# Key and value projections of a second cross-attention in row tiles, pass ends reordered, a last softmax divided late

## The chip, the cores and the metric

The kernel runs on one core of a Trainium2 chip. A core has TensorE (matrix products, results in PSUM), VectorE, ScalarE and GpSimd, and SyncE, whose queue issues most of the transfers from memory. In the profile they are PE (PEld is the loading of weights into TensorE), DVE, ACT, POOL and SP. Every engine runs its own list of instructions in order and waits for others by semaphores. The metric is the device time of one execution in microseconds (us).

## What is computed

`x` is 128 latent rows of 256; the context `ctx` has 12544 rows of 192. Six blocks follow each other, each added to `x`:

```
x = x + cross_attention_0(layernorm(x), ctx)   # 16 heads of 16, then an MLP
x = x + causal_attention(layernorm(x))
x = x + experts_0(layernorm(x))                # 8 experts, top 2
x = x + cross_attention_1(layernorm(x), ctx)   # 16 heads of 64
x = x + attention_1(layernorm(x))
x = x + experts_1(layernorm(x))                # 8 experts, top 2
```

The change is in the fourth and fifth. The fourth is

```
q, k, v = x @ Wq, ctx @ Wk, ctx @ Wv           # Wq 256x1024, Wk and Wv 192x1024
sim  = einsum('bhid,bhjd->bhij', q, k) * 64**-0.5
out  = einsum('bhij,bhjd->bhid', softmax(sim), v)
return out @ Wo + bo
```

and the fifth is

```
probs = softmax(x @ x.T / 16)
vac   = where(probs < 0.01, probs, 0)
sp    = probs - vac;  sp = sp / (sum(sp) + 1e-9)
return sp @ x + 0.01 * (sum(vac) broadcast to 256) @ W.T
```

All of it is float32.

## The kernel before

The context is taken in 13 superblocks of 1024 rows (the last has 256). In the second cross-attention (`with tc.tile_pool(name="l1x"...)`, from L898) two heads make a pass, so there are 8 passes. A period is one superblock of one pass, 104 in all: `periods[t] = (j, s)`. A period projects the keys of its superblock (192 rows of weights to 128 columns, two heads), computes the scores of all 1024 keys with 128 queries and two heads, and keeps them in SBUF; 14 periods later (`LAG`), when the pass's maximum is known, they are shifted by the maximum, exponentiated, summed, and multiplied with the values, which are projected shortly ahead.

The 192 rows of the contraction do not fit TensorE's 128 rows. `load_context` brings the first 128 rows as one tile `lo` (1024 columns), and the last 64 as a tile `hi`, whose upper 64 partitions hold the first half of the superblock's columns and whose lower 64 the second half. `project_keys` and `project_values` work on two PSUM banks, one for each half `r` of the superblock. `tiled()` multiplies the 64 rows of `hi`: two products on the two 64-row halves of the array, side by side, one for each bank (L213 for keys, L231 for values). `whole(r)` multiplies the 128 rows of `lo` on the whole array, one bank after the other (L216, L238). `ahead` says which of the two starts the accumulation. Keys come as two products of 512 columns a half, values as products of 128 columns. In the profile each float32 product is two instructions, so x32 at L980 are 16 products, that is 8 pairs of heads.

Most periods are run two at a time by `two_periods(t)`, for t = 12, 14, ... 100, under a manual schedule: the order in which its calls are written is each engine's order. A call handles, on TensorE: attention of the two periods that are 14 back (`attend`, L1098, on 128x64 tiles), scores of t (`scores`, L980, on 64-row tiles), projections of keys for t + 1 and values, scores of t + 1, with a second set of projections for t + 2 between them. The first set is tiled and then whole, the second whole and then tiled. Beside it: `keeping` gives the copy of the scores to SBUF (L997, ScalarE) and the running maximum (L1004, VectorE); `shift` adds the negative maximum (L1071, GpSimd, or VectorE when `beside`); `exponent` is L1082 on ScalarE; `added` sums over keys on VectorE (L1125) and adds these on GpSimd (L1130) through a ring of three `part` tiles; `taken` adds attention's product to an accumulator (L1142). Keys are copied out of PSUM in halves, half 0 by VectorE (L953) and half 1 by ScalarE (L951), and values by ScalarE (L965).

PSUM holds two double banks for scores and a ring of four single banks (`ps_w`) for all else here: two for keys, two for values, and those of attention, of the transposes at the end of a pass and of the sums. A tile takes a bank that was given back, so the product waits for the reader before it.

At the end of a pass, `fold` reduces the running maximum (L1034, VectorE), `pass_maximum` transposes it (L249) and reduces it again, and `pass_spread` transposes it back over the partitions (L254), into a bank which ScalarE copies to SBUF (L1051) and from which VectorE's `shift` reads directly. The end of a pass falls in the first half of a double (`ends`) or in the second (`ends_later`, followed by a double that `begins`). In the double that begins, the first attention of the new pass used a scores' bank (`late`).

Weights of keys and values for all passes are loaded at the start by `context_weight` (`ywk`, `ywv`), 1024 columns each. A context load is three issues on SP's queue (L194, L196) into two rotating buffers, in the tail every third one into slots of a ring of 28 tiles.

After the last scores comes a tail (t = 104 to 117), in which a period is attention (into `final["both"]`), a projection of values and the exponentials. At t = 107 four products with `ones` and `awT` (L1327) compute the column sums of W that the next block needs. That block (from L1411) runs on one tile: its softmax is divided, masked, summed, divided again, transposed and multiplied. Then the experts (from L1454) follow, whose weights are 24 loads of 512 KB into ring slots.

## Time and profile before

| what | value |
|---|---|
| median of 4 runs | 1570.05 us (1568.65 to 1574.32) |
| profiled execution | 1571.0 us, span 1569.3 us |
| PE busy | 1487.4 us, 95% of the span |
| DVE, ACT, POOL busy | 1156.8, 987.4, 858.2 us |
| mean granted clock of TensorE | 0.989 |
| mean DMA throughput | 93 GB/s |

The second cross-attention begins at about 571 us of the span and ends at about 1505; its paired periods run from 616 to 1426 us. A line of the timeline gives the start in us from the span's beginning, the length, the engine, the line of the kernel, the operation, what it writes and reads, its shape, how many such instructions follow each other, and in brackets the idle time of the engine before it with the instruction that ended it. A line of the chain of waits gives start, length, engine, tile and line. Lengths of matrix products include a modelled end that overlaps the next one, so the distance between starts tells what one took.

### The profile page before, as it was taken

How to read it: one execution, taken by the hardware profiler on the slowest of the kernel's cores; microseconds unless marked ns; L12 is line 12 of the kernel's file. 1: busy time of each engine (PE TensorE's matmuls, PEld its weight loads, DVE VectorE, ACT ScalarE, POOL GpSimd, SP SyncE). 2: the span in 40 equal slices, each digit the busy share in tenths (PEclk: the TensorE clock that was granted, in tenths of full speed). 3: DMA queues.
4: the chain of work that ended last, by engine and by line, in shares of the span. 5: the costliest groups of instructions: out<-in, count | busy, mean ns of one | idle time of the engine just before them, and what ended most of it. 6: DMA issues, size and time to landing. Idle time of an engine off the chain costs nothing.

```text
span 1569.3 us, 39688 instructions
## 1 busy us (share of the span) xinstructions
PE 1487.4 (95%) x17138; PEld 1150.8 (73%) x17138; DVE 1156.8 (74%) x1226; ACT 987.4 (63%) x1233; POOL 858.2 (55%) x563
## 2 busy tenths in 40 slices
PE   7999989999879999999999999999999999999979
PEld 4666656666645877887787887787887788888968
DVE  3899887999883327777778876778876878778742
ACT  4899988999883236665565655565655565555541
POOL 0488878988840000763874663864663864764300
PEclk9999999999999999999999999999999999999979
DMA  3111021211086860332223332223322223224680
GB/s 105 44 61 42 27 62 42 62 43 42 14 240 191 267 169 18 98 97 70 82 82 89 96 86 67 81 82 96 93 82 69 80 83 105 82 82 134 186 282 4
DMA packets 68737, 146.62 MB, mean 93 GB/s; under 512 B 8905, under 2 KB 27089, under 8 KB 68562
## 3 DMA queue, kind: packets, MB, share of 16 engines
q1 hardware_dynamic: 68258, 143.30, 31.0%
q8 instruction: 135, 2.21, 0.6%
q10 hardware_dynamic: 304, 0.79, 0.2%
q14 instruction: 40, 0.33, 0.1%
HBM read 143.92 MB, written 0.13 MB: 92 GB/s over the span
## 4 chain that ended last, share of the span: by engine, by line
PE 62%; DVE 7%; ACT 4%; POOL 3%; issue 2%; DMA 1%; DVEq 0%; ACTq 0%
PE x_s L980 11%; PE x_v L238 10%; PE x_k L216 9%; PE x_o L1098 8%; PE x_v L231 5%; PE x_k L213 5%; POOL x_p L1071 2%; PE f_h L1469 2%; PE f_h L842 2%; PE f_py L859 2%; PE x_both L1098 1%; PE k L216 1%; DVE x_part L1125 1%; ACT x_p L525 1%; POOL x_p L514 1%
## 5 line engine op out<-in xcount | busy, mean ns | idle before, releaser
L1071 POOL TENSOR_TENSOR x_p<-x_p,x_spread 128x1024 f32<-128x1024 f32 x179 | 410.2, 2327 | 206.3 <-ACT x_spread L1051 206.3
L514 POOL TENSOR_TENSOR x_p<-x_p,x_spread 128x512 f32<-128x512 f32 (+1 forms) x184 | 324.4, 1812 | 127.0 <-ACT x_spread L502 65.1
L1125 DVE TENSOR_REDUCE x_part<-x_p 128x256 f32<-128x1024 f32 (+1 forms) x175 | 327.9, 1914 | 18.5 <-POOL x_sums L1130 10.4
L997 ACT COPY x_p<-x_s 128x1024 f32<-128x1024 f32 (+1 forms) x200 | 198.9, 1001 | 206.8 <-PE x_s L980 105.4
L1130 POOL TENSOR_TENSOR x_sums<-x_sums,x_part 128x256 f32<-128x256 f32 x161 | 117.4, 729 | 255.2 <-DVE x_part L1125 254.3
L1004 DVE TENSOR_TENSOR x_mx<-x_s,x_mx 128x1024 f32<-128x1024 f32 (+1 forms) x161 | 193.3, 1201 | 79.1 <-PE x_s L980 58.9
L449 ACT COPY x_p<-x_s 128x1024 f32<-128x1024 f32 x196 | 193.5, 1016 | 50.6 <-PE x_s L436 35.5
L238 PEld LDWEIGHTS x_v<-ywv_lo,x_ctx_lo 128*128 128x128 f32 x1568 | 190.0, 192 | 39.6 <-issue 36.1
L1082 ACT ACTIVATE x_p<-x_p 128x1024 f32<-128x1024 f32 (+1 forms) x200 | 204.6, 1048 | 17.8 <-POOL x_p L1071 13.7
L525 ACT ACTIVATE x_p<-x_p 128x1024 f32<-128x1024 f32 x196 | 196.5, 1063 | 0.2 <-DVE x_p L514 0.2
L238 PE MATMUL x_v<-ywv_lo,x_ctx_lo 128*128 128x128 f32 x1568 | 195.4, 276 | 0.2 <-ACT x_v L965 0.2
L455 DVE TENSOR_TENSOR x_mx<-x_s,x_mx 128x1024 f32<-128x1024 f32 x140 | 168.1, 1221 | 33.0 <-PE x_s L436 18.2
L980 PE MATMUL x_s<-x_qT,x_kT 64*128 64x128 f32 x2744 | 175.5, 277 | 11.5 <-ACT x_p L997 9.5
L980 PEld LDWEIGHTS x_s<-x_qT,x_kT 64*128 64x128 f32 x2744 | 161.7, 188 | 21.0 <-ACT x_p L997 11.2
L216 PE MATMUL x_k<-x_ctx_lo,ywk_lo 128*128 128x512 f32 (+1 forms) x364 | 167.3, 582 | 0.0
L1098 PE MATMUL x_o<-x_p,x_v 128*64 128x128 f32 x2744 | 160.9, 274 | 0.1
L1098 PEld LDWEIGHTS x_o<-x_p,x_v 128*64 128x64 f32 x2744 | 148.7, 137 | 6.4 <-issue 0.4
L231 PEld LDWEIGHTS x_v<-ywv_hi,x_ctx_hi 64*128 64x128 f32 x1568 | 104.2, 188 | 42.9 <-issue 41.6
L436 PE MATMUL x_s<-x_qz,x_kT 32*128 32x256 f32 x1568 | 118.6, 403 | 17.7 <-ACT x_p L449 16.6
L965 ACT COPY x_v<-x_v 128x512 f32<-128x512 f32 (+1 forms) x208 | 108.4, 565 | 32.0 <-PE x_v L238 24.5
L538 PE MATMUL x_o<-x_p,x_v 128*32 128x128 f32 x3136 | 113.7, 279 | 9.9 <-ACT x_p L525 9.0
L538 PEld LDWEIGHTS x_o<-x_p,x_v 128*32 128x32 f32 x3136 | 83.1, 110 | 54.3 <-ACT x_p L525 20.0
(268 smaller groups left out, 1788.2 us busy)
## 6 DMA issues: line engine op xcount, KB each, us to landing
x_ctx_lo<-in_ctxT_dram SPq DMA_DIRECT2D x119, 512.0 KB, 4.0
x_ctx_hi<-in_ctxT_dram SPq DMA_DIRECT2D x238, 128.0 KB, 3.9
f_w<-in_L_ffn_W_dram SPq DMA_DIRECT2D x32, 512.0 KB, 5.1
k_lo<-in_ctxT_dram SPq DMA_DIRECT2D x12, 512.0 KB, 8.5
f_gating<-n_kernel_gating_EDF_dram SPq DMA_DIRECT2D x8, 512.0 KB, 10.4
f_up<-L_ffn_kernel_up_EDF_dram SPq DMA_DIRECT2D x8, 512.0 KB, 10.0
f_wd<-ffn_kernel_down_EFD_dram SPq DMA_DIRECT2D x8, 512.0 KB, 10.1
k_hi<-in_ctxT_dram SPq DMA_DIRECT2D x24, 128.0 KB, 7.7
```

The source lines that it names most:

```text
L216: nc.tensor.matmul(ps[r][:, :h], wk[0][:, js], lo[:, r * h : (r + 1) * h], start=not ahead, stop=ahead)
L238: nc.tensor.matmul(ps[r][:, kc * P : (kc + 1) * P], lo[:, r * h + kc * P : r * h + (kc + 1) * P], wv[0][:, js], start=(not ahead and kc == ...
L449: nc.scalar.copy(ps[t][k], st[k].rearrange("p a n -> p (a n)"))
L514: engine.tensor_tensor(v, v, by[:, banks].unsqueeze(2).to_broadcast([P, n, 2, 256]), ALU.add)
L525: nc.scalar.activation(ps[t][k], ps[t][k], AF.Exp)
L538: nc.tensor.matmul(os[b][32 * i : 32 * i + 32, u * P : (u + 1) * P], v[:, 2 * g + c, 17 * (2 * i + u) : 17 * (2 * i + u) + 32], p[i // 2][ ...
L980: nc.tensor.matmul(st[:, u, c * P : (c + 1) * P], kTs[t][rs, ks], qT[rs, j, :], start=True, stop=True)
L997: nc.scalar.copy(scores_kept(ps[t][i], sts[i].shape[2] // P), sts[i])
L1071: engine.tensor_tensor(v, v, by.unsqueeze(2).to_broadcast([P, 2, n, P]), ALU.add)
L1082: nc.scalar.activation(v, v, AF.Exp)
L1098: nc.tensor.matmul(o[us, 0:P], vs[t][:, c0 + c, us], p[:, n0 : n0 + P], start=(c0 + c == 0 and (s == 0 or not whole)), stop=(c0 + c == tot ...
L1125: nc.vector.tensor_reduce(part, v, AX.X, ALU.add)
```

## The change

Projections of keys and values in the second cross-attention are made wholly of 64-row products. A context tile now has 128 partitions of three pieces: the upper 64 partitions hold the 192 rows of the first half of the superblock as three pieces of 64, the lower 64 those of the second half. A projection has three steps; in a step, the two halves are multiplied side by side, each on its half of the array and into its own bank. Context tiles rotate through three buffers, in the tail too. Weights are loaded by pass, both halves of the partitions holding the same three pieces, one pass ahead.

In the double periods the first set's keys and then values run whole, the second set's too; the copies of keys out of PSUM are placed anew. In the doubles that end or begin a pass, `pass_maximum` and `pass_spread` stand between keys, the first step of values, and the other two; a second shift is done by VectorE; sums of exponentials are placed later; `fold` of the doubles that end later is moved to the next one; the late attention uses an ordinary bank after the second values. The column sums of W leave the tail and are computed after the attention's residual, into a bank of their own. In the next block the masked probabilities are transposed and multiplied before their division, which comes with the last addition; the discarded part is computed by GpSimd.

```
+    def load_rows(t, ap):
+        nc.sync.dma_start(t, ap.rearrange("(c p) n -> p c n", p=64))
+
+    def load_context_rows(pool, name, s, bufs):
+        k0 = s * SB
+        h = min(SB, SK - k0) // 2
+        t = pool.tile([P, 3, KB], F32, tag="ctx", name=name, bufs=bufs)
+        for r in range(2):
+            load_rows(t[64 * r : 64 * r + 64, :, :h], a["ctxT"][:, k0 + r * h : k0 + (r + 1) * h])
+        return t, h
+
+    def project_keys_in_rows(name, w, cx):
...
+        def go(i):
+            for r in range(2):
+                rs = slice(64 * r, 64 * r + 64)
+                nc.tensor.matmul(ps[r][:, :h], w[rs, i, :], t[rs, i, :h], start=(i == 0), stop=(i == 2))
...
+    def project_values_in_rows(name, w, cx):
...
+        def go(i):
+            for kc in range(h // P):
+                ks = slice(kc * P, (kc + 1) * P)
+                for r in range(2):
+                    rs = slice(64 * r, 64 * r + 64)
+                    nc.tensor.matmul(
+                        ps[r][:, ks], t[rs, i, ks], w[rs, i, :], start=(i == 0 and kc == 0), stop=(i == 2),
...
-        ywk = context_weight(work, "ywk", a["L1_xattn_Wk"])
-        ywv = context_weight(work, "ywv", a["L1_xattn_Wv"])
+        def load_pass_weight(kind, j):
+            if j < NH // 2 and (kind, j) not in weights:
+                t = work.tile([P, 3, P], F32, tag="yw" + kind, name=f"yw{kind}{j}", bufs=2)
+                for r in range(2):
+                    load_rows(t[64 * r : 64 * r + 64], a["L1_xattn_W" + kind][:, j * P : (j + 1) * P])
+                weights[kind, j] = t
...
-            place = slot if t >= NP and (t - NP) % 3 == 2 else None
-            ctxs[t] = load_context(work, f"x1_ctx{t}", (t + 1) % NS, 2, place=place)
+            ctxs[t] = load_context_rows(work, f"x1_ctx{t}", (t + 1) % NS, 3)
...
+            if begins:
+                fold(j)
             context(t)
...
-            k[0]()
-            v[0]()
+            whole(k)
             copy, maximum = keeping(t, sts)
             copy(0)
             if begins or ends:
...
+                out(k)
                 pass_maximum(j)
-                v[1](0)
+                whole(v, 0)
                 pass_spread(j)
-                v[1](1)
-                for r in range(2):
-                    v[2](r)
-                first, second = (b[1], nx) if begins else (nx[0], nx[1:])
-                shift(first, 0, True)
-                shift(first, 1)
-                for u in second:
-                    shifted(u)
-                exponents(first)
-                if begins:
-                    summed(2, first)
-                    exponents(nx[0])
-                    summed(1, nx[0])
-                else:
-                    summed(3, first)
+                whole(v, 1, 2)
+                out(v)
+                first = [(u, i) for u in (b[1:] + nx if begins else nx) for i in range(2)]
+                for i in (0, 2):
+                    shift(*first[i], True)
+                for u, i in first:
+                    shift(u, i)
+                for u, i in first[:2]:
+                    exponent(u, i)
             else:
-                for f in (k, v):
-                    for r in range(2):
-                        f[1](r)
+                whole(v)
...
+            k, v = keys(t + 2), values(t + 2 - NS)
+            whole(k)
+            if ends:
+                summed(2, nx[0])
+                exponent(nx[1], 0)
+                out(k)
+                summed(1, nx[1])
+            elif begins:
+                summed(2, b[1])
+                exponent(nx[0], 0)
+                out(k)
+                exponent(nx[0], 1)
+                summed(1, nx[0])
+            else:
+                out(k)
+            whole(v)
             if begins:
-
-                late = attend(b[1], ps_s(f"x1_o{b[1]}")[:, 0])
...
+                o = attend(b[1])
+                taken(b[1], o)
+            out(v)
+            if not begins and not ends and at != NS - 3:
                 summed(1)
...
                 if t == NP + 3:
-
-                    for c in range(2):
-                        nc.tensor.matmul(
-                            final["both"][:, 1, D : 2 * D], ones, awT[:, c, :], start=(c == 0), stop=(c == 1)
-                        )
                     projected(0, PASSES - 1)
...
-            wsum = final["both"][:, 1, D : 2 * D]
+            pc = ps_mm("a1_pc")
+            for c in range(2):
+                nc.tensor.matmul(pc[:, :D], ones, awT[:, c, :], start=(c == 0), stop=(c == 1))
...
         sp = work.tile([P, P], F32, name="a1_sp")
-        nc.vector.tensor_tensor(sp, pr, vac, ALU.subtract)
+        nc.vector.scalar_tensor_tensor(sp, pr, 0.01, pr, ALU.is_ge, ALU.mult)
+        pt = ps_t("a1_spT_ps")
+        nc.tensor.transpose(pt[:, 0:P], sp, ident)
...
-        spn = work.tile([P, P], F32, name="a1_spn")
-        nc.vector.tensor_scalar(spn, sp, rs, None, ALU.mult)
-        spT = transposed(work, spn, 1, "a1_spT", tag="spT")
+        spT = work.tile([P, P], F32, name="a1_spT")
+        nc.vector.tensor_copy(spT, pt[:, 0:P])
...
+        nc.gpsimd.tensor_tensor(vac, pr, sp, ALU.subtract)
...
+        x = xp.tile([P, D], F32, tag="x", name="x5")
+        nc.vector.scalar_tensor_tensor(x, pa[:, :D], rs, y, ALU.mult, ALU.add)
```

## The prediction

> **What bounds the kernel now.** I read the page first: busy times, then the chain that ended last.
>
> ```profile
> PE 1487.4 (95%) x17138; PEld 1150.8 (73%) x17138; DVE 1156.8 (74%) x1226; ACT 987.4 (63%) x1233; POOL 858.2 (55%) x563
> PE 62%; DVE 7%; ACT 4%; POOL 3%; issue 2%; DMA 1%; DVEq 0%; ACTq 0%
> ```
>
> TensorE is the bound, and the changed attention (571 to 1505 us of the span) is most of it. Next I read TensorE's timeline of one ordinary double (two periods by `two_periods`): start, length, engine and line, tiles.
>
> ```profile
> 1034.53 2.06 PE L980 MATMUL x_s<-x_qT,x_kT 64*128 64x128 f32 x32
> 1036.42 1.03 PE L213 MATMUL x_k<-x_ctx_hi,ywk_hi 64*128 64x512 f32 x4
> 1037.28 1.06 PE L231 MATMUL x_v<-ywv_hi,x_ctx_hi 64*128 64x128 f32 x16
> 1038.26 1.98 PE L216 MATMUL x_k<-x_ctx_lo,ywk_lo 128*128 128x512 f32 x4
> 1040.09 1.95 PE L238 MATMUL x_v<-ywv_lo,x_ctx_lo 128*128 128x128 f32 x16
> 1041.87 1.88 PE L216 MATMUL x_k<-x_ctx_lo,ywk_lo 128*128 128x512 f32 x4
> 1043.59 1.95 PE L238 MATMUL x_v<-ywv_lo,x_ctx_lo 128*128 128x128 f32 x16
> 1045.47 1.13 PE L213 MATMUL x_k<-x_ctx_hi,ywk_hi 64*128 64x512 f32 x4
> 1046.43 1.06 PE L231 MATMUL x_v<-ywv_hi,x_ctx_hi 64*128 64x128 f32 x16
> 1047.32 1.95 PE L980 MATMUL x_s<-x_qT,x_kT 64*128 64x128 f32 x32
> 1049.20 3.71 PE L1098 MATMUL x_o<-x_p,x_v 128*64 128x128 f32 x64
> ```
>
> No idle time is noted and the next double starts at 1052.85: 18.32 us, all TensorE. Lengths include a tail that the next group overlaps, so I use the distances between starts. Where kinds of tile change, a group costs about 0.1 more: values in rows 0.89 (1046.43, scores follow) but 0.98 ahead of a whole one; keys in rows 0.86 (1036.42) but 0.96 after a whole one; whole keys 1.72 or 1.83; whole values 1.78 or 1.88. Then the ends of passes, in the chain of waits, and TensorE's waits at an end in the timeline:
>
> ```profile
> 979.57 8.20 POOL x_p L1071 x4
> 988.88 2.37 POOL x_p L1071
> 991.97 1.97 DVE x_part L1125
> 996.23 2.83 PE x_s L980 x32
> ```
>
> ```profile
> 1087.48 1.93 DVE L1034 TENSOR_REDUCE x_folded<-x_mx 128x256 f32<-128x1024 f32 x1
> 1090.06 0.44 PE L249 MATMUL x_mt<-ident,x_folded 128*128 128x128 f32 x2 [0.31 <-DVE x_kT L953]
> 1092.05 1.22 DVE L1071 TENSOR_TENSOR x_p<-x_p,x_mb 128x1024 f32<-128x1024 f32 x1 [1.09 <-ACT x_spread L1051]
> ```
>
> In the first, five shifts on GpSimd delay a sum, that the maxima, and these the scores: TensorE idles 2.5 us before 996.23. In the second the fold sets when the transposes go. Last the tail, one period, and the end's softmax:
>
> ```profile
> 1488.00 1.16 PE L231 MATMUL x_v<-ywv_hi,x_ctx_hi 64*128 64x128 f32 x16
> 1489.10 2.05 PE L238 MATMUL x_v<-ywv_lo,x_ctx_lo 128*128 128x128 f32 x16
> 1491.08 1.97 PE L1098 MATMUL x_both<-x_p,x_v 128*64 128x128 f32 x32
> 1513.68 0.45 PE L156 MATMUL a_spT_ps<-ident,a_spn 128*128 128x128 f32 x1 [3.96 <-DVE a_spn L1442]
> ```
>
> **The change part by part.** The sum is made against the profiled execution: 1571.0 us, span 1569.3; the median of the runs is 1570.05.
>
> *Ordinary doubles.* There are 45 doubles from period 12 on: 4 end a pass in their first half, 3 in their second, 3 begin one, 35 are ordinary. Now 1036.42 to 1047.32 is 10.90 us of projections. After, all is row pairs beside the scores' own mode. Keys: 6 pairs a period at 0.86 / 2 = 0.43, 2.58. Values: 24 pairs at 0.89 / 8 = 0.111, 2.67. Twice: 10.50, so 0.40 less, 14.0 over 35. The pair rate holds over 16 pairs in the scores (1.88, entry to the next mode included), so 24 should hold it; bounds 0.2 (the longer runs lose half) to 0.45. The waits near it stay covered: counted from the scores' start, the second keys begin at 1.89 + 2.58 + 2.67 = 7.14, and their banks are read out by 5.6 on VectorE and 6.4 on ScalarE (1039.43 and 1040.34 plus their lengths); the second values begin at 9.7, ScalarE's copies of the first run from about 7.3 to 8.4 (1.07). If that cover of 0.7 went, each 0.1 would cost 4.5.
>
> *Four doubles that end a pass.* From the first scores (1085.38): keys in rows end at 0.54 + 2.58 = 3.1, the fold at 4.0 as now, so the transposes start at 4.15 (now 4.68) after 1.0 idle. The first step of values needs keys' half 0 copied out after the fold: 4.0 + 0.7, start 4.85. Its 0.89, the spread's transposes (0.22) and changes of mode that were none among whole tiles (about 0.1 each) put the other two steps at 6.3 to 8.1. Each step of row pairs needs both banks of its target at once, and the second keys' half 1 gets the bank of the spread, that two shifts on VectorE read (now one): transposes 5.9, ScalarE's copy to 6.7, two of 1.22 to 9.2. Then 9.3 + 2.58 + 2.67 = 14.6, scores, attention and the sums as now (1097.79 to 1103.54, 5.75): 20.35 against 18.16 now. +2.2 each, +8.8. Bounds +0.7 (changes of mode alone) to +4 (another 1.8 for values waiting behind exponentials).
>
> *Three that begin one.* From 970.95 to the next double's scores is 25.28. The fold moves in here, behind one small maximum: keys end at 5.0, transposes follow at once, values wait 0.3 for a bank, spread 7.0, two shifts to 10.3, second keys 10.4 to 13.0 after 1.1 idle, values to 15.6. VectorE has two sums (1.96 each) before it copies keys out at 16.2, and attention's bank waits for that: 0.6. Scores at 18.3, attention of two 20.2 to 23.8, sums 24.1. The sums that GpSimd held back now stand behind the maxima, and GpSimd has four shifts, done at 17.5, not five: the 2.5 us idle goes. 24.1 against 25.28: -3.6 in all. Bounds -5.3 (also the clock: 0.72 granted after 996.23, where 14.45 stands for 12.79; 763.45 and 1230.67 show 1.00) to +1.5.
>
> *Around them.* Three doubles with a short second half: -0.2 each, -0.6 (0.4 less, short keys' copy waits again). Seven doubles after an end carry one more sum ahead of the keys' copy: 7.2 against 7.14, 0.15 each, +1.0.
>
> *Tail.* A period is 1.10 + 1.98 + 1.89 = 4.97; after 24 pairs 2.67 + 0.2 for both changes of mode + 1.89 = 4.76, eleven times: -2.3. Four matmuls leave it (1454.10 to 1455.06), -0.9, and stand under layernorm's 2.26 us wait before 1507.33: free.
>
> *Last softmax.* From 1511.70 to the next layernorm's 1516.81 is 5.11. After: masking 0.32, transpose starts 0.11 later and takes 0.49, copy 0.34 (the reduce, add and reciprocal, 0.7, lie beside it), matmul 1.26, combining 0.51: 3.1. GpSimd's subtraction and three small VectorE steps end within the matmul. -2.0; bounds -1.4 to -2.3.
>
> *DMA.* Context comes in two issues of 384 KB, 2 KB rows, instead of 512 + 2 x 128 KB, weights in four of 96 KB a pass instead of 2 MB at the start. Three buffers give a load 18 us or more from release to use in doubles, 9 in the tail; a landing takes 4.0 now. SP's queue has 1.43 us of issues a period now, so the weights ahead of a context load delay it by 2 at most. Nothing. The last stage's weights start one period later (1484.65 now, done by 1520) and are first wanted at about 1518, by expert 0 alone: nothing.
>
> Sum: -14.0 + 8.8 - 3.6 - 0.6 + 1.0 - 2.3 - 0.9 - 2.0 = -13.6 on 1571.0, 1557.4; against the median 1556.5. I say 1557.
>
> **Two rules of the Trainium skill.** The trace has VectorE's shift set when a row step's second bank is free. "TensorEngine Tiling (Array Packing)", Restrictions and Gotchas, says why this speaks against the change: different row tiles write different banks, so tiling in rows raises PSUM pressure, and its Key Properties say that a change of mode drains the array, which the 0.1 above agrees with. By the page alone the sum has the sign of these two only, no size. On the clock, the row is 0.72 after a 2.5 us idle in one case of three. "TensorE: Matmul & The Clock Gate", Part 1, wants a whole idle window of about 3.4 us first; by the page the new idles of 1.0 to 1.2 cost nothing, and the sum stays at -13.6; by the row's one bad case at all seven ends (7 x 1.66) it would be -2.0.
>
> **Rivals.**
> *The ends lose the clock* (0.10): idles of 1.0, 0.3 and 1.2 within 6 us add up as the 2.5 did. 1571.0 - 2.0 = 1569, median 1568. Against: two of the three 2.5 us idles did nothing.
> *Row pairs are no faster in long runs* (0.08): the 0.1 belongs to changes of weights, not of mode. -13.6 + 14.0 = +0.4: 1570.5, no change. Against: whole values after whole keys cost 1.72 to 1.78 without it.
> *Both banks at once stall every ordinary double* (0.11): the second keys or values wait for ScalarE, whose queue holds exponentials ahead of the copies. Slower from (13.6 + 4.7) / 35 = 0.5 a double, ScalarE 1.2 later than I place it; at 0.7 it is -13.6 + 24.5 = +10.9: 1582. For it: the cover is 0.7 only. Against: in the double shown ScalarE itself waits 0.43 for the keys, so it would be earlier.
> *My forecast* has 0.71.
>
> **How the numbers follow.** A measurement tells about 0.3% (4.7 us) here. Faster: 0.71 and a third of the clock rival (other sizes of it), 0.74. Same: the rest of that, the second rival: 0.15. Slower: 0.11. The forecast's own bounds: ordinary -7.0 to -15.8, ends +2.8 to +16, begins -5.3 to +1.5; not all at one end, so 1548 to 1565 for it. Range 1548 to 1569 takes in the clock rival.
>
> **What would show it.** Right: no line of whole projections after 616 us; ordinary doubles at 17.9; ends at about 20.3, their second keys waiting for VectorE's shift; begins at 24, no wait of 2.5 before scores; tail periods 4.76; 3.1 in the softmax. Wrong: an idle before keys or values in ordinary doubles, a granted clock under 0.9 at ends, or pairs of values above 0.12 us.

## The result, and the profile after

The changed kernel takes 1573.63 us (median; 1568.27 to 1580.74), the kernel before 1571.29 us beside it (1565.74 to 1577.4). The ratio is 1.0018, 95% interval 1.0012 to 1.0024. That is 0.2% longer, far less than single executions of either kernel differ; 1557 us was forecast, 0.9% less. The profiled execution took 1571.57 us with a span of 1569.8 us (before: 1571.0 and 1569.3).

The page of the changed kernel, busy times, the DMA queue of SP (packets, MB, share of 16 engines), and the chain's shares by engine:

```profile
PE 1486.7 (95%) x19070; PEld 1162.0 (74%) x19070; DVE 1160.2 (74%) x1231; ACT 980.5 (62%) x1233; POOL 842.4 (54%) x557
...
q1 hardware_dynamic: 85538, 144.14, 36.8%
...
PE 62%; DVE 6%; DMA 4%; ACT 4%; issue 1%; POOL 1%; SPq 0%; DVEq 0%; ACTq 0%
```

Two things differ from before. GpSimd's share of the chain fell from 3% to 1%, and DMA's rose from 1% to 4%. The queue moved about the same bytes (143.30 MB before) in a quarter more packets (68258 before), and took 36.8% of the engines' time where it took 31.0%.

An ordinary double is what it was forecast to be. TensorE's timeline of the changed kernel (start, length, engine, line, operation, tiles, shape, count):

```profile
1047.28 2.06 PE L1031 MATMUL x_s<-x_qT,x_kT 64*128 64x128 f32 x32
1049.17 2.74 PE L263 MATMUL x_k<-x_ctx,ywk 64*128 64x512 f32 x12
1051.75 2.84 PE L277 MATMUL x_v<-ywv,x_ctx 64*128 64x128 f32 x48
1054.43 2.74 PE L263 MATMUL x_k<-x_ctx,ywk 64*128 64x512 f32 x12
1057.00 2.85 PE L277 MATMUL x_v<-ywv,x_ctx 64*128 64x128 f32 x48
1059.68 1.95 PE L1031 MATMUL x_s<-x_qT,x_kT 64*128 64x128 f32 x32
1061.56 3.71 PE L1149 MATMUL x_o<-x_p,x_v 128*64 128x128 f32 x64
1065.21 1.05 PE L1031 MATMUL x_s<-x_qT,x_kT 64*128 64x128 f32 x14
```

No wait is noted; from 1047.28 to 1065.21 are 17.93 us, where it was 18.32. Keys take 2.57 from start to start, values 2.68. The time that these doubles gained is lost again later, in the tail. The same view there:

```profile
1455.26 1.97 PE L1149 MATMUL x_both<-x_p,x_v 128*64 128x128 f32 x32
1457.16 2.95 PE L277 MATMUL x_v<-ywv,x_ctx 64*128 64x128 f32 x48
1460.04 1.97 PE L1149 MATMUL x_both<-x_p,x_v 128*64 128x128 f32 x32
1467.41 0.76 PE L277 MATMUL x_v<-ywv,x_ctx 64*128 64x128 f32 x2 [5.41 <-DMA x_ctx<-in_ctxT_dram]
1469.47 5.46 PE L277 MATMUL x_v<-ywv,x_ctx 64*128 64x128 f32 x46 [1.30 <-DMA x_ctx<-in_ctxT_dram]
1474.86 1.98 PE L1149 MATMUL x_both<-x_p,x_v 128*64 128x128 f32 x32
...
1482.12 0.46 PE L277 MATMUL x_v<-ywv,x_ctx 64*128 64x128 f32 x2 [0.51 <-DMA x_ctx<-in_ctxT_dram]
1484.14 4.52 PE L277 MATMUL x_v<-ywv,x_ctx 64*128 64x128 f32 x46 [1.55 <-DMA x_ctx<-in_ctxT_dram]
```

The first period (1455.26 to 1460.04) takes 4.78, as forecast. Then values wait for their context 5.41 and 1.30 us, and the 46 products that follow take 5.39 us from start to start, about twice their time: the granted clock from 1467.41 to 1474.86 is 0.50. It happens again at 1484. The waits of this line add up to 10.2 us. SP's issues in the same stretch (SPq; the length of a line with several issues runs from the start of the first to the end of the last):

```profile
1450.62 3.55 SPq L245 DMA_DIRECT2D x_ctx<-in_ctxT_dram  x2
1455.24 0.64 SPq L64 DMA_DIRECT2D f_up<-L_ffn_kernel_up_EDF_dram  x1
1456.97 1.66 SPq L245 DMA_DIRECT2D x_ctx<-in_ctxT_dram  x2
1460.03 0.37 SPq L64 DMA_DIRECT2D f_wd<-ffn_kernel_down_EFD_dram  x1
1463.16 1.41 SPq L64 DMA_DIRECT2D f_gating<-n_kernel_gating_EDF_dram  x1
1465.54 2.35 SPq L245 DMA_DIRECT2D x_ctx<-in_ctxT_dram  x2
```

Between the context loads stand loads of the last stage's weights. Before the change the first of them was issued at 1484.65, behind the last context; now it is at 1433.67. SP's lines of before, then of the changed kernel:

```profile
1483.45 1.10 SPq L196 DMA_DIRECT2D x_ctx_hi<-in_ctxT_dram  x2
1484.65 0.53 SPq L64 DMA_DIRECT2D f_gating<-n_kernel_gating_EDF_dram  x1
```

```profile
1433.67 0.37 SPq L64 DMA_DIRECT2D f_gating<-n_kernel_gating_EDF_dram  x1
```

The context that TensorE waits for at 1467.41 was issued at 1450.62, as soon as its buffer was free, its second half at 1453.57; they took 16.7 and 15.8 us to land. The one that TensorE waits for at 1482.12 was also issued late: its buffer was free at about 1460, but it comes at 1465.54, behind two weight loads. The engines in this stretch (columns: busy us and instructions of PE, PEld, DVE, ACT, POOL; granted clock, DMA share, GB/s):

```profile
1440.00:1460.00 20.00, 19.64 (x290) 17.90 (x287) 16.37 (x15) 8.97 (x13) 17.71 (x8) 1.00 1.06 272
1460.00:1480.00 20.00, 13.30 (x168) 12.26 (x168) 7.95 (x8) 6.14 (x9) 0.00 (x0) 0.74 1.06 220
1480.00:1500.00 20.00, 16.55 (x238) 15.18 (x234) 9.47 (x9) 8.73 (x13) 0.00 (x0) 0.91 1.08 244
```

The DMA share adds up the times of packets, which can overlap, so it can pass 1. It is above 1 throughout, and yet the engines move 220 to 272 GB/s; when only weights ran, before the change, they moved 375 (1490 to 1504 us).

Stage by stage, from the two traces (e1 is the first experiment below; the last projection is attention's output projection, with `ywo`):

| stretch | before | after | difference | e1 |
|---|---|---|---|---|
| to the first scores | 578.91 | 578.74 | -0.2 | 580.04 |
| doubles that end a pass (4) | 74.8 | 84.2 | +9.4 | |
| doubles that begin one (3) | 75.8 | 71.6 | -4.3 | |
| second halves of the three that end later | | | -0.4 | |
| 35 ordinary doubles | | | -13.8 | |
| scores of period 102 to the last projection | 77.02 | 90.28 | +13.3 | 74.19 |
| last projection to the first expert product | 16.95 | 14.21 | -2.7 | 13.94 |
| from there to the end of the span | 48.6 | 47.9 | -0.7 | 47.4 |

The paired doubles gained 9.1 us and the end 3.4; the tail took 13.3.

### The profile page after: what moved, and what is told of

Same layout as the page of the kernel before. It is cut to its first block, busy times and chain, and to the rows that moved or that the text cites. A ratio compares the mean times of both kernels' runs of the same rounds, so it can differ in the third digit from the quotient of the medians.

```text
span 1569.8 us, 43441 instructions
## 1 busy us (share of the span) xinstructions
PE 1486.7 (95%) x19070; PEld 1162.0 (74%) x19070; DVE 1160.2 (74%) x1231; ACT 980.5 (62%) x1233; POOL 842.4 (54%) x557
## 3 DMA queue, kind: packets, MB, share of 16 engines
q1 hardware_dynamic: 85538, 144.14, 36.8%
## 4 chain that ended last, share of the span: by engine, by line
PE 62%; DVE 6%; DMA 4%; ACT 4%; issue 1%; POOL 1%; SPq 0%; DVEq 0%; ACTq 0%
PE x_v L277 15%; PE x_k L263 13%; PE x_s L1031 11%; PE x_o L1149 10%; DMA x_ctx<-in_ctxT_dram 3%; PE f_h L1511 2%; PE f_h L881 2%; PE f_py L898 2%; ACT x_p L564 1%; PE k L213 1%; DVE x_part L1176 1%; DMA f_gating<-n_kernel_gating_EDF_dram 1%; POOL x_p L553 1%; PE f_py L1549 1%; DVE x_mx L494 1%
## 5 line engine op out<-in xcount | busy, mean ns | idle before, releaser
L1122 POOL TENSOR_TENSOR x_p<-x_p,x_spread 128x1024 f32<-128x1024 f32 (+1 forms) x172 | 394.1, 2324 | 206.0 <-ACT x_spread L1102 206.0
L277 PEld LDWEIGHTS x_v<-ywv,x_ctx 64*128 64x128 f32 x4704 | 292.2, 192 | 50.5 <-issue 45.7
L277 PE MATMUL x_v<-ywv,x_ctx 64*128 64x128 f32 x4704 | 299.4, 277 | 10.2 <-DMA x_ctx<-in_ctxT_dram 10.2
L263 PE MATMUL x_k<-x_ctx,ywk 64*128 64x512 f32 (+1 forms) x1092 | 245.2, 568 | 0.9 <-DVE x_kT L1004 0.6
L263 PEld LDWEIGHTS x_k<-x_ctx,ywk 64*128 64x128 f32 x1092 | 103.1, 187 | 81.8 <-issue 74.2
```

Source lines behind the costliest of these rows:

```text
L263: nc.tensor.matmul(ps[r][:, :h], w[rs, i, :], t[rs, i, :h], start=(i == 0), stop=(i == 2))
L277: nc.tensor.matmul(ps[r][:, ks], t[rs, i, ks], w[rs, i, :], start=(i == 0 and kc == 0), stop=(i == 2), skip_group_check=True,)
L1122: engine.tensor_tensor(v, v, by.unsqueeze(2).to_broadcast([P, 2, n, P]), ALU.add)
```

## The experiments

**e1: the last stage's weights behind the last context.** Only the order on SP's queue changes:

```
-        gu = [
+        with tc.issue_after(issued["last"]):    # the last context load
+            gu = [
...
```

> The changed kernel, with one thing held: the 24 loads of the last stage's weights are issued on SP's queue behind the last context load, as they were before the change. Nothing is left out. Theory O (the loads want more than the DMA engines give): in the changed kernel's tail a period wants 0.786 MB of context, at the 225 GB/s that its ordinary doubles show for a full engine share (90 GB/s at a share of 0.40), 3.5 us, and two slots' worth of weights, 1.05 MB at 375 GB/s, 2.8 us: 6.3 us in a period of 4.77. With the weights held back contexts alone want 3.5, so the 10.2 us of waits go and the throttled clock with them: tail from the last scores to the last projection 74 us as predicted (90.3 in the changed kernel, 77.0 before), the whole at about 1555 to 1558 us, 0.990 to 0.992 of the kernel before. Rival S (the shape alone: two transfers of 2 KB rows land too late for periods of 4.77, whatever else is on the queue): at least 5 us of waits for contexts stay, 1562 to 1570 us. Rival L (the weights now come too late): no waits in the tail, but the last stage waits for its weights, 1560 us or more.

Measured: 1557.42 us, ratio 0.9905 (0.9889 to 0.9921). The tail from TensorE's timeline and the first weights on SP's queue:

```profile
1458.85 2.95 PE L279 MATMUL x_v<-ywv,x_ctx 64*128 64x128 f32 x48
1461.73 1.97 PE L1151 MATMUL x_both<-x_p,x_v 128*64 128x128 f32 x32
1463.63 2.95 PE L279 MATMUL x_v<-ywv,x_ctx 64*128 64x128 f32 x48
1466.51 1.97 PE L1151 MATMUL x_both<-x_p,x_v 128*64 128x128 f32 x32
...
1493.50 0.70 PE L1220 MATMUL x_both<-ywo,x_oT 128*128 128x256 f32 x2 [1.01 <-DVE x_oT L1443]
```

```profile
1457.09 21.32 SPq L247 DMA_DIRECT2D x_ctx<-in_ctxT_dram  x10
1478.51 0.55 SPq L64 DMA_DIRECT2D f_gating<-n_kernel_gating_EDF_dram  x1
```

Every period takes 4.78, no value waits for a context, and the tail takes 74.19 us. The last stage does not wait for its weights either: its products follow each other as before. Theory O's number came out; the shape alone (rival S) and late weights (rival L) are out. So the whole loss of the changed kernel comes with the weights among the tail's contexts: 10.2 us of waits, and products at a low clock behind them.

**e2: the tail's contexts on another queue.** The edit in short:

```
     def load_rows(t, ap, queue=None):
-        nc.sync.dma_start(t, ap.rearrange("(c p) n -> p c n", p=64))
+        (queue or nc.sync).dma_start(t, ap.rearrange("(c p) n -> p c n", p=64))
...
-                    context(t)
+                    context(t + 2)    # queue nc.scalar from t = 104
```

> The changed kernel, but the context loads of the tail (from period 104) are issued by ScalarE on its own queue, each two periods ahead of its use, when the buffer it takes is free; the last stage's weights stay on SP's queue and start as soon as slots are free. Nothing is left out. Theory O (shared engines): the queue is not what the contexts wait for; the 16 engines are as full as before, so TensorE still waits 5 to 12 us for contexts in the tail, 1564 to 1573 us. Rival Q (head of the line: a context stands behind a weight load that waits for its slot): the contexts no longer stand behind them, the waits go, 1555 to 1559 us.

Measured: 1573.45 us, ratio 1.0004 (0.9992 to 1.0017). A queue of their own saved no time. The contexts landed 11.5 us after their issue (median, issues from 1440 to 1490 us) and the weights 13.2. But the waits took another form than theory O had said: only 2.0 us are TensorE's own for contexts, for now ScalarE waited before its issues, and its exponentials stood behind them:

```profile
1485.44 9.12 ACTq L245 DMA_DIRECT2D x_ctx<-in_ctxT_dram  x2
1494.61 2.00 ACT L1133 ACTIVATE x_p<-x_p 128x1024 f32<-128x1024 f32 x2 [10.10 <-DMA x_ctx<-in_ctxT_dram]
```

Each of the two issues takes 0.60 us; the second starts at 1493.96, after a weight load of SP's queue landed at 1493.94 (more on this at e12). TensorE waited 4.95 us for these exponentials, and 4.61 in an earlier period. So the time lost moved, and what the place in the queue costs by itself this run does not tell. The Trainium skill, "DMA: Bandwidth & Descriptors", section "Rules for kernel authors", says that spreading transfers over issuing engines brings no bandwidth, as all run on the same 16 DMA engines. The time agrees; the throughput from 1440 to 1490 us was 273 GB/s against 242 in the changed kernel, with more weights in the mix.

**e3: the tail's contexts in their old shape.** Their values are projected as before, too. Weights stay between the contexts on SP's queue in nearly the same order, the first of them issued at 1433.83.

```
+            nc.sync.dma_start(lo[:, :n], a["ctxT"][0:P, k0 : k0 + n])
+            for r in range(2):
+                nc.sync.dma_start(hi[64 * r : 64 * r + 64, :h], a["ctxT"][P:C, k0 + r * h : k0 + (r + 1) * h])
```

> The changed kernel, but in the tail (from period 104) the contexts are loaded as before the change, one piece of 128 rows with 4 KB rows and two of 64, and the values are projected tiled and whole; weights are still interleaved with the contexts on SP's queue, and there are still three buffers. Nothing is left out. Theory O: at the 290 GB/s of the old shape (87 GB/s at a share of 0.30 in ordinary doubles) a period's context wants 2.7 us and the weights 2.8: 5.5 in a period of 4.97, so the excess falls from 1.5 us a period to 0.5 and most of it is covered by the loads made ahead: waits of 0 to 5 us, tail 78 to 83 us, 1558 to 1564 us. Rival Q (the place in the queue alone): the waits stay at about 10 us, and the tail is longer by the old 0.2 a period, 1570 to 1575 us.

Measured: 1558.82 us, ratio 0.9913 (0.9893 to 0.9933). No value waits for a context; weights and contexts together move faster at the same full share:

```profile
1440.00:1460.00 20.00, 20.00 (x229) 18.00 (x226) 16.83 (x16) 9.43 (x13) 17.80 (x8) 1.00 1.00 301
1460.00:1480.00 20.00, 20.00 (x260) 18.35 (x259) 14.45 (x13) 12.41 (x17) 0.00 (x0) 1.00 1.05 293
```

So either remedy is enough: the weights alone would not have hurt the old loads, and the new loads alone (e1) fit into the shorter periods. It takes both.

**e4: the last softmax alone, on the kernel before.** The edit is the diff's part from `pr` on, with the four products of `awT` behind the residual.

> The kernel before, with only the end's softmax changed (masked probabilities transposed and multiplied before their division, column sums of W moved behind the residual). Nothing is left out. Prediction's step: 2.0 less for the softmax and 0.9 less for the four products that leave the tail: 2.9 less, 0.9982 of the kernel before. Rival: the stage that follows waits for its weights instead (the transfers end at about 1520 us of the span, its first product starts at 1520.7), so the gain is given back: 0.9995 to 1.0.

Measured: 1567.84 us, ratio 0.9973 (0.9961 to 0.9984), that is 2.5 to 6.1 us less; in its trace the last projection to the first expert product takes 13.98 us, not 16.95. The rival is out: the first expert product does not wait for weights.

**e5: the changed kernel with loads of 128 partitions.** e6, e7 and e10 ask the same question of the kernel before.

```
-        for r in range(2):
-            load_rows(t[64 * r : 64 * r + 64, :, :h], a["ctxT"][:, k0 + r * h : k0 + (r + 1) * h])
+        for c in range(3):
+            nc.sync.dma_start(t[:, c, :h],
+                a["ctxT"][64 * c : 64 * c + 64, k0 : k0 + 2 * h].rearrange("p (r n) -> r p n", r=2))
```

> The changed kernel, but every context of the second attention is loaded in three issues of 128 partitions (both halves of one piece, 256 KB), not in two of 64 partitions (three pieces of one half, 384 KB). The rows are 2 KB as they were, their places and the products are the same, weights stay interleaved with contexts on SP's queue. Nothing is left out. Theory P (transfers to 64 partitions are what costs): from the shares of ordinary doubles, 0.30 with two thirds of the bytes to 128 partitions and 0.40 with all to 64, a MB costs 47 us of one engine to 128 partitions and 73 to 64; so the share in ordinary doubles falls to 0.26, a context in the tail wants 2.3 us, with the weights 5.1 in a period of 4.77, which the loads made ahead cover: waits of 0 to 2 us, 1555 to 1559 us, 0.990 to 0.992 of the kernel before. Rival R (rows of 2 KB, 50 KB apart in memory, are what costs): the share stays at 0.40 and the waits at about 10 us, 1571 to 1575 us.

Measured: 2287.99 us, ratio 1.4559 (1.4538 to 1.458). Both theories missed. All through the second attention TensorE waits for contexts, while the DMA engines seem idle:

```profile
1300.00:1700.00 400.00, 278.76 (x3058) 207.62 (x3058) 182.00 (x162) 137.26 (x180) 138.85 (x94) 0.81 0.14 51
```

A share of 0.14 is little more than 2 of 16 engines (0.125). The Trainium skill, "DMA: Bandwidth & Descriptors", section "Rules for kernel authors", gives a cause: the number of engines of a transfer follows the size of the outermost dimension of its patterns. Here that is the source's r, which is 2. The trace agrees with 2 engines; that the two halves' order is the cause was not tried otherwise. The run says nothing on 64 against 128 partitions.

**e6, e7, e10: other shapes of the 128-row piece, in the kernel before.** In the paired periods it is loaded in two pieces of 128 partitions and 2 KB rows (e6), two of 64 partitions and 4 KB rows (e7), four of 64 partitions and 2 KB rows (e10). The edit of e10; e6 has only its loop over r, with all 128 partitions, and e7 only its loop over c, with all columns:

```
-        queue.dma_start(lo[:, :n], a["ctxT"][0:P, k0 : k0 + n])
+        for c in range(2):
+            for r in range(2):
+                rs, cs = slice(64 * c, 64 * c + 64), slice(r * h, (r + 1) * h)
+                queue.dma_start(lo[rs, cs], a["ctxT"][rs, k0 + r * h : k0 + (r + 1) * h])
```

> The kernel before, but the 128-row piece of every context in the paired periods is loaded in two issues of 128 partitions with 2 KB rows, not in one with 4 KB rows. Nothing is left out. Theory P (64 partitions): the DMA share in ordinary doubles stays at 0.30 (up to 0.32). Rival R (rows of 2 KB): 0.40, as in the changed kernel, for then all rows are of 2 KB. The time stays as it is in both, 1571 us, since nothing waits for contexts there.

> The kernel before, but the 128-row piece of every context in the paired periods is loaded in two issues of 64 partitions each, with its 4 KB rows. Nothing is left out. Theory P (64 partitions): the DMA share in ordinary doubles rises to 0.40, for then all transfers go to 64 partitions. Rival R (rows of 2 KB): it stays at 0.30. The time stays at 1571 us.

> The kernel before, but the 128-row piece of every context in the paired periods is loaded in four issues of 64 partitions with 2 KB rows. Nothing is left out. Shares from 700 to 1390 us so far: 0.30 as it was, 0.28 with 128 partitions and 2 KB rows, 0.33 with 64 partitions and 4 KB rows, 0.40 in the changed kernel (64 partitions, 2 KB rows, three pieces an issue). Theory H (64 partitions and short rows together): 0.37 to 0.40. Rival I (what more the changed kernel shows comes from three pieces in one issue): 0.32 to 0.34. The time stays at 1571 us.

One execution of each: 1571.59, 1573.54 and 1570.2 us, no change, as all had expected. DMA shares from 700 to 1390 us:

| loads | share | GB/s |
|---|---|---|
| before: 128 partitions, 4 KB (two thirds of the bytes) | 0.30 | 85 |
| e6: 128 partitions, 2 KB | 0.28 | 85 |
| e7: 64 partitions, 4 KB | 0.33 | 85 |
| e10: 64 partitions, 2 KB | 0.29 | 85 |
| after: 64 partitions, 2 KB, three pieces in one issue | 0.40 | 89 |

Rival R (short rows) fell with e6. In e7 neither theory's number came out; theory P (64 partitions) and theory H fell with e10, which lies even below rival I's 0.32 to 0.34. What is left of the differences is the issue of three pieces.

**e12: the changed kernel with six issues to a context.**

```
-        for r in range(2):
-            load_rows(t[64 * r : 64 * r + 64, :, :h], a["ctxT"][:, k0 + r * h : k0 + (r + 1) * h])
+        for c in range(3):
+            for r in range(2):
+                cols = slice(k0 + r * h, k0 + (r + 1) * h)
+                nc.sync.dma_start(t[64 * r : 64 * r + 64, c, :h], a["ctxT"][64 * c : 64 * c + 64, cols])
```

> The changed kernel, but every context of the second attention is loaded in six issues of 64 partitions and one piece (128 KB), not in two of three pieces (384 KB). Partitions, rows and their places are the same; weights stay interleaved with contexts on SP's queue. Nothing is left out. The looks at the kernel before gave DMA shares of 0.28 to 0.33 for all shapes of one piece an issue, 64 partitions with 2 KB rows among them (0.29), and the changed kernel 0.40. Theory I (three pieces in one issue are what costs): the share from 700 to 1390 us falls to 0.28 to 0.32, a context in the tail wants about 2.6 us, with the weights 5.4 in a period of 4.77, mostly covered by loads made ahead: waits of 0 to 3 us, 1555 to 1561 us. Rival C (the shares only show how much is under way at once; with full engines 64 partitions and short rows are slow in whatever issues): the waits stay at 5 to 12 us, 1565 to 1574 us.

Measured: 1563.67 us, ratio 0.9934 (0.9906 to 0.9962), between the two theories; the share is 0.31 at the same 89 GB/s, as theory I said, and 5.8 us of waits are left, which lie in rival C's range. The landing times in the tail (issues from 1440 to 1483 us: KB each, median us from issue to landing) tell the rest. Changed kernel, then e12:

```profile
x_ctx<-in_ctxT_dram SPq DMA_DIRECT2D x12, 384.0 KB, 15.8
f_gating<-n_kernel_gating_EDF_dram SPq DMA_DIRECT2D x4, 512.0 KB, 16.9
```

```profile
x_ctx<-in_ctxT_dram SPq DMA_DIRECT2D x40, 128.0 KB, 6.6
...
f_gating<-n_kernel_gating_EDF_dram SPq DMA_DIRECT2D x4, 512.0 KB, 6.8
```

With one piece an issue, contexts land after 6.6 us instead of 15.8, and the weights among them also faster. Without weights (e1) the three-piece issues land after 5.6, as they do in the doubles. What e12 still waits for is, by its trace, late issue: a context whose buffer was free at 1464.56 was issued at 1467.46, behind a weight load that SP issued only at 1467.00, and the six issues took 3.7 us of SP's time. So one piece an issue shortens the landing, and the place in the queue counts too, here as for the changed kernel's context of 1465.54.

The traces also show what an issue waits for, and that suggests why landings take so long. All loads take turns on eight semaphores, and each waits until the load eight places before it has landed. In the changed kernel from 1437 to 1500 us, 17 of the 27 issues for which this can be read start within 0.1 us of that landing (1453.57 after 1453.55, 1465.54 after 1465.48); in e12 from 1437 to 1495, 11 of 51 (1467.00 after 1466.93); in the kernel before from 700 to 1390 us, none of 174. In e2 the loads of both queues share these eight. So with full engines a load can have seven others beside it. If it lands after the time that eight take, by the mean size of the issues from 1440 to 1483 us and the throughput there, that is an estimated 8 x 442 KB at 243 GB/s, 14.9 us, in the changed kernel, and 8 x 217 KB at 269 GB/s, 6.6 us, in e12; 15.8 and 6.6 were measured. By this estimate most of e12's shorter landing comes of the smaller loads. No run changed the number of loads under way, so it fits but is not shown; why three pieces take the larger share and move fewer bytes stays open.

**e8: one shift by VectorE at the ends, on e1.**

```
-                for i in (0, 2):
+                for i in (0,):
                     shift(*first[i], True)
```

> The kernel of the first run (weights of the last stage held back), but in the doubles that end or begin a pass VectorE does one shift from the spread's bank, as before the change, and GpSimd all others. Nothing is left out. The prediction's step (the second keys wait for the bank that VectorE's second shift reads): an end takes 18.9 to 19.4 us, not 20.15, and a begin 22.6 to 23.2, not 23.85; about 6 us less in all. Rival: the second keys start when the first values end, and only their last products wait for the bank; GpSimd's extra shift (2.35 us) makes an exponential and a sum late instead: an end takes 19.9 to 21, a begin 23.8 to 26, where GpSimd again holds the sums ahead of the maxima.

One execution: 1551.23 us. A double that ends a pass takes 19.0 us instead of 20.14 at three of the four; one that begins a pass 23.83 instead of 23.85 at two of the three. The step was right for the ends; in the begins something else took its place (e11). TensorE's timeline of one end, first in e1, then in e8:

```profile
1086.78 2.06 PE L279 MATMUL x_v<-ywv,x_ctx 64*128 64x128 f32 x32
1088.67 3.46 PE L265 MATMUL x_k<-x_ctx,ywk 64*128 64x512 f32 x11
1091.58 0.60 PE L279 MATMUL x_v<-ywv,x_ctx 64*128 64x128 f32 x4
1091.97 0.59 PE L265 MATMUL x_k<-x_ctx,ywk 64*128 64x512 f32 x1
```

```profile
1083.56 2.06 PE L279 MATMUL x_v<-ywv,x_ctx 64*128 64x128 f32 x32
1085.44 2.74 PE L265 MATMUL x_k<-x_ctx,ywk 64*128 64x512 f32 x12
1088.02 2.85 PE L279 MATMUL x_v<-ywv,x_ctx 64*128 64x128 f32 x48
```

In e1 the wait hides: no idle time is noted, but 11 products take 3.46 us, and values begin (1091.58) before the last product of the keys (1091.97). In e8 the 12 products take 2.74 as in an ordinary double.

**e9 and e11: both mended, and keys copied out earlier.** e9 is e8's kernel, in five executions. e11 changes this on it:

```
             elif begins:
+                out(k)
                 summed(2, b[1])
                 exponent(nx[0], 0)
-                out(k)
                 exponent(nx[0], 1)
```

> The kernel of the run with one shift by VectorE and the last stage's weights held back, timed. Nothing is left out. Theory (the held weights give 14 us, the bank freed earlier 1.14 at each of three ends and some 2 more around): 1551 to 1554 us, 0.987 to 0.989 of the kernel before. Rival (the one look was 5 us lucky; ends gain 1.1 each and no more): 1554 to 1557, 0.989 to 0.991.

> The kernel with both mended, but in the three doubles that begin a pass the second keys are copied out ahead of the two sums and the exponential that stood before them. Nothing is left out. The prediction's step (VectorE has two sums before it copies keys out, and attention's bank waits for that): in the trace of the mended kernel attention waits 1.47 us there, so a begin takes 22.3 to 22.8 us, not 23.83, 3 to 4.5 us less in all, 0.2 to 0.3%. Rival (the sums, now later, hold the maxima, and these the scores that follow, as GpSimd did before the change): 23.6 to 25 us.

Measured: e9 1552.14 us, ratio 0.9866 (0.9844 to 0.9888); e11 1548.91 us, ratio 0.984 (0.9813 to 0.9866). The intervals overlap, but the traces show e11's gain where it was expected: the three doubles that begin a pass take 22.65, 22.29 and 22.29 us instead of 24.65, 23.81 and 23.84. The two profiled executions as wholes hardly differ (1550.95 and 1550.68 us): e11's reached the scores ahead of its doubles 6.7 us later (610.49 against 603.79), with a granted clock of 0.94 instead of 0.99 from 420 to 600 us, where the two kernels are the same. The late attention of one such double on TensorE, in e9 and then in e11:

```profile
977.84 2.85 PE L279 MATMUL x_v<-ywv,x_ctx 64*128 64x128 f32 x48
982.13 1.97 PE L1151 MATMUL x_o<-x_p,x_v 128*64 128x128 f32 x32 [1.45 <-ACT x_p L1135]
```

```profile
981.41 2.84 PE L279 MATMUL x_v<-ywv,x_ctx 64*128 64x128 f32 x48
984.18 1.97 PE L1151 MATMUL x_o<-x_p,x_v 128*64 128x128 f32 x32
```

In e9 attention waits 1.45 us. The profile names ScalarE's exponential (980.97 plus 1.06), which ends when VectorE's copy of the keys does (981.32 plus 0.67); but in e11 attention starts at 984.18 and that exponential at 984.55, so it was the bank that the copy frees. This is why e8 gained nothing here: with the second shift the changed kernel waits for the spread's bank first and 0.35 us for this one; without it, the second keys are earlier and the whole wait is at the attention. e11 has the lowest median here, 1.6% below the kernel before.

## Why the prediction was wrong

| term | predicted | measured |
|---|---|---|
| 35 ordinary doubles, with the 7 after an end | -14.0 + 1.0 | -13.8 |
| four doubles that end a pass | +8.8 | +9.4 |
| three that begin one | -3.6 | -4.3 |
| three short second halves | -0.6 | -0.4 |
| tail, with the four products that leave it | -2.3 - 0.9 | +13.3 (-2.8 in e1) |
| last softmax | -2.0 | -2.7 |
| DMA | nothing | the tail's 16 |

**The step that failed** is the last sentence of the paragraph on DMA, and with it the term that the sum puts at nothing: it was 16.1 us (a tail of 90.28 against 74.19 in e1). "The last stage's weights start one period later" was wrong by 51 us in the other direction: they start at 1433.67, not after 1484.65. By the code, the diff's line without `place=slot` is the reason: before, every third context of the tail took two tiles of the ring of 28; now none does, and the last stage's loads, which take slots of the same ring, are placed between the contexts. e3, with the old shape but without these slots, has the first weights at 1433.83 too; no run puts the slots back, so this part is read and not tried. The prediction read that line as a third buffer for contexts and did not ask who takes the slots it gives back. "Three buffers give a load [...] 9 in the tail; a landing takes 4.0 now" then failed with it: in the tail a landing took 15.8 us, with issues of three pieces beside weights (e12), and one context was issued some 5 us after its buffer was free. e1 and e3 show that each half alone is harmless.

With the weights held back the sum of the prediction is met: 1557.42 us against 1557, the tail -2.8 against -3.2. Part of that is luck: the -13.8 of the ordinary doubles holds 1.66 us that the kernel before lost to a low clock in one double (19.98 against 18.32). Without it they gained 12.2, where 13.0 was forecast.

**What was right.** The rate of row pairs: 2.57 and 2.68 a group, 0.39 or 0.40 less in the doubles away from the ends. The end of a pass, with its mechanism: 20.15 measured at three of four against 20.35, of which e8 measured 1.14 for the bank that the second shift reads, where the prediction had put 1.2 (9.3 instead of 8.1). The fourth, the first end (t = 12), lost 3.4: there TensorE idles 3.17 us for the fold, and the granted clock from 622 to 625 us is 0.50 (before the change 2.69 us and 1.00). The begins: 23.85 against 24.1, GpSimd's 2.5 us idle ahead of the scores gone, and attention's wait for the keys' copy there (0.35 in the changed kernel against 0.6). Of the seven doubles after an end five gained 0.16 to 0.18 (0.25 predicted); another gained 1.83, as the kernel before had run it at a low clock. Three more doubles, each the second after a begin, gained only 0.13 to 0.15, which the prediction did not foresee. The softmax's copy and transposition, by e4 as by the changed kernel, gave a little more than forecast.

Of the two rules that the prediction weighed, the one on the clock ("TensorE: Matmul & The Clock Gate", Part 1) agrees with most rows: over three of the ends, with 0.87 us idle, the granted clock was 1.00; after 5.41 us in the tail it was 0.50. The first end does not fit it: after 3.17 us, less than the page's whole window, the clock was 0.50 as well.

```profile
622.30 0.69 PE L288 MATMUL x_mt<-ident,x_folded 128*128 128x128 f32 x2 [3.17 <-DVE x_folded L1085]
```

The one on PSUM ("TensorEngine Tiling (Array Packing)", Restrictions and Gotchas) has its price here: 1.14 us at an end and 1.5 at a begin, both for a bank that VectorE gave back late (e8, e11). Of the three rivals, two (row pairs no faster, banks that stall ordinary doubles) did not happen. The one on the clock came at one end of the four, and after one long idle, not several short ones. None of the three had looked at the tail.

## What to carry to other kernels

When a change gives a shared buffer back, ask which transfers were waiting for it: they move forward, and what they meet there may be the stage that was just made shorter. Cost a load in the stretch where it runs, by bytes over the throughput seen in its own shape with what runs beside it, and not by its landing time in a quieter stage; ask also how many loads may be under way at once, and how large those ahead of it are. A wait in row tiles may leave no idle time in the profile; a group that is longer than its twin elsewhere shows it.

## What the runs showed of the hardware

- Context loads of the same bytes, partitions and row lengths took a DMA share of 0.40 in issues of 64 partitions by three pieces and 0.31 in issues of one piece; beside weight loads they landed after 15.8 and 6.6 us (e12), which an estimate from eight loads under way at once also gives (14.9 and 6.6).
- Loads whose source pattern has an outermost dimension of 2 moved 51 GB/s at a share of 0.14 (e5).
- Rows of 2 KB were no dearer than rows of 4 KB (0.28 against 0.30, e6), and 64 partitions alone little (0.33 and 0.29, e7 and e10).
- In this program a load was issued only when the load eight places before it had landed; ScalarE's exponentials stood behind such a wait of nearly 8 us between two issues of 0.60 (e2). An issue itself took 0.60 us, with a DMA share above 1 once 2.58 (changed kernel, 1450.62).
- The granted clock fell to 0.50 after 3.17 us of idle TensorE (changed kernel, 622.30) and stayed at 1.00 after 2.69 at the same place (kernel before).
